# A two-layer block on one core: down products one chunk later, the second batch's norm ahead of the first mixer, attention's additions behind a gated value

## The chip, the cores and the metric

The kernel runs on one core of a Trainium2 chip. The metric is device time in microseconds (us) for one execution. The kernel before takes 360.51 us (median of three runs, 360.42 to 360.6). TensorE (PE in the profile) multiplies matrices, VectorE (DVE) and ScalarE (ACT) do elementwise work, GpSimd (POOL) does a few small powers, SyncE (SP) issues nearly all the DMAs.

## The reference

Four batches of 512 rows of 256 values pass through two layers. Each layer is a layer norm, a "mixer" `s` and a feed-forward `g` that start from the same normed value, and `x + s * silu(g)`.

```python
xn = _layernorm(x)
s = _L0_attn_ref(xn, ...)        # one step of a linear recurrence from zero state, RMS norm, + xn
g = _silu(_L0_ffn_ref(xn, W1, W2, W3))
x = x + s * g
xn = _layernorm(x)
s = _L1_attn_ref(xn, ...)        # layer norm, causal softmax attention, output projection, + xn
g = _silu(_L1_ffn_ref(xn, W1, W2, W3))
x = x + s * g

def _ffn_ref(x, W1, W2, W3):     # hidden size 1024, both layers
    hidden = silu(x @ W1.T) * (x @ W3.T)
    return fwht(hidden) @ W2.T   # Walsh-Hadamard transform of the hidden values
```

## The kernel before

**Precision.** Every matrix operand is kept as a high and a low part (`hi` cast by ACT at L61, `lo = src - hi` by DVE at L62, in `split`). A product is then three products, high by high, high by low and low by high; `mm3` (L80) issues them. So each value that goes into a product costs one ACT cast and one DVE subtraction, and the low part is always the last to come.

**Layer 0.** Batches are numbered 0 to 3 here, as in the code. For each batch `ffn` (L461) runs over eight chunks of 128 hidden values: two up products into PSUM (names `f_<b>gu`, a gate and a linear one, a pool of three banks), silu on ACT (L522), the product of the two on DVE (L523, name `f_<b>h`, called the gate of the chunk here; it frees the bank of the linear product), a split into `f_<b>hh` and `f_<b>hl`, and `down`, whose twelve products per chunk accumulate in `f_<b>dn`. `down` of a chunk is issued `defer` chunks after its up products; `defer` is 1 for batches 1 to 3 and 8 for batch 0, where the weights of the down product are still being prepared. In the program text the up and down products stand one after the other, and a `Beside` object puts steps of other work into 16 slots between them: the mixer of the same batch, the norm and transposes of the next batch, the gate of the batch before, the preparation of weights.

`mixer(b)` (L709) multiplies the transposed normed value with one 256 by 256 matrix (tiles `o`, four blocks, two to a bank), copies and squares on ACT (L719, L721), takes the power on POOL (L724), scales four tiles on DVE (L726, names `osb`) and adds them into `xn` (L729). The layer's output is made by `gate`: silu of the down products (L692, names `g_<b>g`), times `xn` (L698), added to `x` (L700). `norm(0, b + 1)` reads the next batch, makes `xn`, transposes it on PE (`xt_<b>tp`) and splits it into `xt`.

**Who decides the order.** In layer 0 the order of the instructions on each engine is chosen by the framework's scheduler from its own estimates, with the program order and the explicit `after(...)` links as inputs. Each engine then runs its list strictly in that order, and waits on semaphores for what the others deliver. From the end of layer 0's last up product the order of PE is fixed by hand (`line["fixed"]`).

**Layer 1.** `ffn_s` (L556) does the up products of two hidden chunks at a time, in four steps `q`, in a Strassen-like scheme of seven block products into banks `g`, `l` and `z` (names `f_<b>gu<q>g` and so on; the same pool of three banks). At the end of a step ACT takes silu of `g` into `h0`, and DVE multiplies it with `l` (L668, `first["gate"]`), which frees the bank that the next step's `z` needs. Attention's parts stand between the block products in a hand-written list of places. `pv` (L853) multiplies softmax weights with values; after every second tile it adds two tiles of the result into `xn` on DVE (L871). `prep_s` loads weights, makes sums of blocks, splits them (names `sraw`, `ssum`, `sp`) and stores them to DRAM, from where `load_s` reads them back (`sw`).

Of the kernel before, what the change touches and what calls it, by code (L numbers as in the profile page):

```python
# [35 lines left out]
def kernel(ctx: ExitStack, tc: tile.TileContext, a: dict, out: bass.AP):  # L36
    nc = tc.nc
# [39 lines left out]
    def transpose(*args):  # L77
        return in_line(nc.tensor.transpose, *args)

    def mm3(o, terms):  # L80

        seq = [(l[0], r[0]) for l, r in terms]
        for l, r in terms:
            seq += [(l[0], r[1]), (l[1], r[0])]
        for n, (l, r) in enumerate(seq):
            ins = matmul(o, l, r, start=n == 0, stop=n == len(seq) - 1)
        return ins
# [128 lines left out]
    def sl(i):  # L216
        return slice(i * P, (i + 1) * P)
# [72 lines left out]
    def k_pairs(lhs, lcols, rhs, rcols):  # L290
        return [
            ((lhs[0][:, k, lcols], lhs[1][:, k, lcols]), (rhs[0][:, k, rcols], rhs[1][:, k, rcols]))
            for k in range(2)
        ]
# [166 lines left out]
    def ffn(name, xT, w13, w2, slot, defer=1, spare=(), parts=1, behind=False, tail=()):  # L461

        w2h, w2l = w2
        dn, outs, firsts = [], [], {}

        def down(c, hh, hl, tiles=range(NT)):
            if not dn:  # L470
                dn.extend(psum(f"{name}dn{i}", [P, 2, D], tag="dn", bufs=2) for i in range(2))
                outs.extend(dn[t // 2][:, t % 2, :] for t in range(NT))
            for t in tiles:
                o = outs[t]
                for n, (l, r) in enumerate(((hh, w2h), (hh, w2l), (hl, w2h))):
                    first = c == 0 and n == 0
                    stop = c == NH - 1 and n == 2

                    def one(start):
                        return matmul(  # L480
                            o, l[:, sl(t)], r[:, c, :], start=start, stop=stop, skip_group_check=True
                        )

                    if first and t % 2 == 1:
                        with tc.issue_after(firsts[t // 2].ins):
                            ins = one(False)
                    elif first:
                        ins = firsts[t // 2] = one(True)  # L490
                    else:
                        ins = one(False)
            return ins

        queue, gates, late = [], [], []
        for c in range(NH):
            with after(gates[-2] if behind and c >= 2 else None):
                wh, wl = w13(c // 2)
            gu = []
            for j in range(2):  # L500

                o = psum(f"{name}gu{c}_{j}", [P, S], **(DN[0] if behind and c == 1 else GU))
                cols = slice((c % 2) * D + j * P, (c % 2) * D + (j + 1) * P)
                gu.append((o, cols))
            for half in range(parts if c == 0 else 1):
                n = S // (parts if c == 0 else 1)
                ts_ = slice(half * n, (half + 1) * n)
                if parts == 1 or c:
                    for o, cols in gu:
                        last_up = mm3(o[:, ts_], k_pairs((wh, wl), cols, xT, ts_))  # L510
                    continue

                for n, (w, x) in enumerate(((wh, xT[0]), (wl, xT[0]), (wh, xT[1]))):
                    for o, cols in gu:
                        for k in range(2):
                            last_up = matmul(
                                o[:, ts_], w[:, k, cols], x[:, k, ts_],
                                start=n + k == 0, stop=n + k == 3,
                            )
            gu = [o for o, _ in gu]  # L520
            h = hid(f"{name}h{c}")
            first["silu"] = nc.scalar.activation(h, gu[0], AF.Silu)  # L522
            gates.append(nc.vector.tensor_tensor(h, h, gu[1], ALU.mult))  # L523
            first["gate"] = gates[-1]
            if c < len(spare):
                hh, hl = spare[c]
            else:
                hh = hid(f"{name}hh{c}", F32R)
                hl = hid(f"{name}hl{c}", F32R)
            if c < len(spare):  # L530
                nc.scalar.copy(hh, h)
                late.append((hl, h, hh))
            else:
                split(h, hh, hl)
            for _ in range(2 if c >= NH - 2 else 0):
                if late:
                    lo_, h_, hi_ = late.pop(0)
                    with after(gates[-1]):
                        nc.vector.tensor_tensor(lo_, h_, hi_.bitcast(F32), ALU.subtract)
            queue.append((c, hh, hl))  # L540
            ups = last_up if behind else None
            with after(gates[-1] if behind else None), after(ups):
                slot(2 * c)
            if len(queue) > defer:
                down(*queue.pop(0))
            with after(gates[-1] if behind else None), after(ups):
                slot(2 * c + 1)
        line["fixed"] = bool(tail)
        line["last"] = last_up
        for what in tail:  # L550
            what()
        for q in queue:
            down(*q)
        return dn
# [154 lines left out]
    def mixer(b):  # L709

        xn, xT, m = xns[0, b], xTs[0, b], first["m"]
        osb = t4(f"osb{b}", [P, NT, D])
        r = small(f"ssr{b}")
        junk = t2(f"junk{b}", [P, D])
        for i in range(2):
            o = psum(f"o0_{b}_{i}", [P, 2, D])
            for j in range(2):
                mm3(o[:, j, :], k_pairs(xT, sl(2 * i + j), m, ALLD))
            nc.scalar.copy(osb[:, 2 * i : 2 * i + 2, :], o)  # L719
            for t in (2 * i, 2 * i + 1):  # L720
                nc.scalar.activation(junk, osb[:, t, :], AF.Square, accum_out=r[:, t : t + 1])  # L721
            yield
        nc.vector.tensor_scalar(r, r, 1.0 / D, RMS_EPS, ALU.mult, ALU.add)
        nc.gpsimd.tensor_tensor(r, r, mhalf, ALU.pow)  # L724
        for t in range(NT):
            nc.vector.scalar_tensor_tensor(  # L726
                osb[:, t, :], osb[:, t, :], r[:, t : t + 1], nwb, ALU.mult, ALU.mult
            )
        nc.vector.tensor_tensor(xn, xn, osb, ALU.add)  # L729
        yield  # L730

    class Attention:
# [45 lines left out]
        def tq(self, j):  # L778
            b = self.b
            if j == 0:  # L780
                self.tqs = t4(f"tqh{b}", [P, 2, S], F32R), t4(f"tql{b}", [P, 2, S], F32R)
            o = psum(f"tq{b}_{j}", [P, S])
            mm3(o, k_pairs(first["wqk"], sl(j), self.xg, ALLS))
            split(o, self.tqs[0][:, j, :], self.tqs[1][:, j, :])

        def v(self, i, j):
# [66 lines left out]
        def pv(self, i):  # L853
            b, xn, pr = self.b, self.xn, self.prs[i]
            if i == 0:
                self.rden = small(f"rden{b}")
                with after(first["h1"]):
                    nc.vector.reciprocal(self.rden, self.den)
            if i % 2 == 0:
                self.o = psum(f"pv{b}_{i}", [P, 2, D])  # L860
            o = self.o[:, i % 2, :]
            mm3(
                o,
                [
                    (tuple(z[:, sl(j)] for z in pr), tuple(z[:, j, :] for z in self.vs))
                    for j in range(i + 1)
                ],
            )
            if i % 2:
                for t in (i - 1, i):  # L870
                    nc.vector.scalar_tensor_tensor(  # L871
                        xn[:, t, :], self.o[:, t % 2, :], self.rden[:, t : t + 1], xn[:, t, :],
                        ALU.mult, ALU.add,
                    )

    class Beside:

# [119 lines left out]
    for b in range(B):  # L997
# [4 lines left out]
            tasks.append((prep, 12))  # L1002
        if b:
            tasks.append((call(gate_all, f"g0_{b - 1}", dn, xns[0, b - 1], xs[b - 1]), 1))
        tasks.append((mixer(b), MIXER))
        if b + 1 < B:
            if b:
                load_x(b + 1)
            if b == 2:
                tasks.append((prep_s(0), 4))  # L1010
            tasks.append((norm(0, b + 1), NORM))
        if b == 0:
            early = w2_tile("early0"), w2_tile("early1")
            spare = [
# [18 lines left out]
        if b == 0:  # L1033
            dn = ffn("f0_0", xTs[0, 0], w13, w2, bg.slot, NH, spare, parts=2, behind=True)
        else:
            tail = [run(atts[0].tq, j) for j in range(2)] if b + 1 == B else []
            dn = ffn(f"f0_{b}", xTs[0, b], w13, w2, bg.slot, tail=tail)
        bg.finish()


# [146 lines left out]
```

## Time and profile before

| | |
|---|---|
| median of three runs | 360.51 us (360.42 to 360.6) |
| the profiled execution | 360.78 us, its span 359.0 us |
| PE busy | 352.4 us (98%), 2477 instructions |
| DVE busy | 287.5 us (80%), 597 instructions |
| ACT busy | 197.8 us (55%), 373 instructions |
| POOL busy | 20.8 us (6%), 22 instructions |
| DMA | 52.25 MB, mean 146 GB/s |

The span is the time from the first to the last instruction that the profile shows; 1.78 us of the profiled execution lie around it. The profiled execution is 0.27 us above the median. Names in the profile have some of their numbers left out: `f_1gu` is batch 1 of layer 0, `f_1gu2z` is bank `z` of step 2 of batch 1 of layer 1. The busy time of consecutive instructions overlaps: two DVE instructions of 0.68 us each can start 0.60 us apart.

### The profile page before, as it was taken

The numbers are of one execution on the slowest core, as the hardware profiler recorded it, in microseconds if no ns is written. First come the engines' busy times: TensorE is split into PE (matmuls) and PEld (weight loads), VectorE is DVE, ScalarE is ACT, GpSimd is POOL, SyncE is SP. The second block draws the span as 40 slices with busy tenths as digits, with TensorE's granted clock in tenths as the row PEclk, the third lists the DMA queues.
The fourth block names the chain that finished last, engine by engine and source line by source line (L and its number), as shares of the span: only waits on it lengthen the run. The fifth ranks groups of instructions, "written<-read, shape, count | busy, mean of one in ns | idle before, by whom it ended". The sixth has DMA issues, their size and how long they took to land.

```text
span 359.0 us, 6278 instructions
## 1 busy us (share of the span) xinstructions
PE 352.4 (98%) x2477; PEld 328.1 (91%) x2477; DVE 287.5 (80%) x597; ACT 197.8 (55%) x373; POOL 20.8 (6%) x22
## 2 busy tenths in 40 slices
PE   8999999999999999999999999999999999999995
PEld 6878998888988898888999999999999999999995
DVE  6899648998579938998886957989669997567645
ACT  3766156266463425674467655576555676556443
POOL 2000110300020210100110001100011000000000
PEclk9999999999999999999999999999999999999999
DMA  7925000301044316656256045572554655445501
GB/s 235 341 91 206 2 1 2 99 18 60 0 157 165 150 39 233 248 180 195 105 207 263 16 190 206 203 224 103 204 179 165 207 186 204 136 151 192 197 2 58
DMA packets 16285, 52.25 MB, mean 146 GB/s; under 512 B 1633, under 2 KB 7937, under 8 KB 16257
## 3 DMA queue, kind: packets, MB, share of 16 engines
q1 hardware_dynamic: 15968, 51.60, 40.9%
q8 instruction: 19, 0.31, 0.4%
q10 hardware_dynamic: 288, 0.26, 0.2%
q14 instruction: 10, 0.07, 0.1%
HBM read 42.40 MB, written 9.45 MB: 144 GB/s over the span
## 4 chain that ended last, share of the span: by engine, by line
PE 96%; DVE 2%; ACT 1%; issue 0%; DVEq 0%
PE f_1dn L70 6%; PE f_2dn L70 6%; PE f_1gu L70 6%; PE f_0gu L70 6%; PE f_2gu L70 6%; PE f_3gu L70 6%; PE f_3dn L70 6%; PE f_0dn L70 6%; PE sc L70 4%; PE pv L70 4%; PE o L70 3%; PE v L70 3%; PE tq L70 3%; PE warm L70 2%; PE w2ps L70 1%; PE pt L70 1%
## 5 line engine op out<-in xcount | busy, mean ns | idle before, releaser
L70 PE MATMUL f_1gu<-xt,w 128*128 128x512 f32 x96 | 24.9, 397 | 0.3 <-ACT xt L61 0.3
L70 PE MATMUL f_3gu<-xt,w 128*128 128x512 f32 x96 | 25.0, 396 | 0.0
L70 PE MATMUL f_2gu<-xt,w 128*128 128x512 f32 x96 | 24.8, 395 | 0.0
L70 PE MATMUL f_0gu<-xt,w 128*128 128x512 f32 (+1 forms) x108 | 24.3, 378 | 0.0
L70 PEld LDWEIGHTS f_0gu<-xt,w 128*128 128x128 f32 x108 | 18.4, 188 | 4.4 <-issue 1.0
L70 PEld LDWEIGHTS f_1gu<-xt,w 128*128 128x128 f32 x96 | 17.0, 188 | 3.6 <-ACT xt L61 0.5
L70 PEld LDWEIGHTS f_2gu<-xt,w 128*128 128x128 f32 x96 | 17.0, 188 | 3.0
L70 PEld LDWEIGHTS f_3gu<-xt,w 128*128 128x128 f32 x96 | 17.0, 188 | 2.9
L61 ACT CAST f_2hh<-f_2h 128x512 fp32r<-128x512 f32 x16 | 9.9, 622 | 15.4 <-DVE f_2h L523 12.3
L70 PE MATMUL f_3dn<-w2l,f_3hh 128*128 128x256 f32 x64 | 17.7, 281 | 0.0
L70 PE MATMUL f_3dn<-w2h,f_3hh 128*128 128x256 f32 x64 | 17.7, 281 | 0.0
L70 PE MATMUL f_1dn<-w2l,f_1hh 128*128 128x256 f32 x64 | 17.7, 282 | 0.0
L70 PE MATMUL f_2dn<-w2h,f_2hh 128*128 128x256 f32 x64 | 17.7, 282 | 0.0
L70 PE MATMUL f_1dn<-w2h,f_1hh 128*128 128x256 f32 x64 | 17.7, 281 | 0.0
L70 PE MATMUL f_2dn<-w2l,f_2hh 128*128 128x256 f32 x64 | 17.6, 281 | 0.0
L70 PE MATMUL f_3dn<-w2h,f_3hl 128*128 128x256 f32 x64 | 17.0, 282 | 0.0
L70 PE MATMUL f_1dn<-w2h,f_1hl 128*128 128x256 f32 x64 | 17.0, 281 | 0.0
L70 PE MATMUL f_2dn<-w2h,f_2hl 128*128 128x256 f32 x64 | 16.7, 281 | 0.0
L61 ACT CAST f_3hh<-f_3h 128x512 fp32r<-128x512 f32 (+1 forms) x17 | 10.0, 594 | 10.2 <-DVE f_3h L523 6.1
L61 ACT CAST f_1hh<-f_1h 128x512 fp32r<-128x512 f32 x16 | 9.9, 622 | 9.7 <-DVE f_1h L523 6.6
L62 DVE TENSOR_TENSOR f_2hl<-f_2h,f_2hh 128x512 fp32r<-128x512 f32 x16 | 10.9, 682 | 3.9 <-ACT f_2hh L61 3.8
L70 PE MATMUL f_0dn<-w2l,f_0hh 128*128 128x256 f32 x48 | 13.7, 286 | 0.0
(487 smaller groups left out, 1147.6 us busy)
## 6 DMA issues: line engine op xcount, KB each, us to landing
sw<-s SPq DMA_DIRECT2D x32, 896.0 KB, 6.4
s<-sp SPq DMA_DIRECT2D x8, 512.0 KB, 3.8
s<-sp SPq DMA_DIRECT2D x8, 384.0 KB, 2.8
w2raw<-in_w SPq DMA_DIRECT2D x4, 512.0 KB, 5.6
sraw<-in_w SPq DMA_DIRECT2D x4, 512.0 KB, 4.3
mrb<-there SPq DMA_DIRECT2D x4, 512.0 KB, 3.7
w13raw<-in_w SPq DMA_DIRECT2D x3, 512.0 KB, 7.1
x<-in_x SPq DMA_DIRECT2D x3, 512.0 KB, 3.6
```

Of the source, the lines that this page charges most:

```text
L61: h = nc.scalar.copy(hi, src)
L62: return h, engine.tensor_tensor(lo, src, hi.bitcast(F32), ALU.subtract)
L70: ins = call(*args, **kwargs)
```

## The change

The change alters no amount of work; the same instructions are issued in another order.

1. `mm3` issued the two low products of each term side by side; now it issues all that use the low part of one operand and then all that use the low part of the other. `late` says which operand's low part comes last: 0 (the default) the left one, 1 the right one. `late=1` is set for the up products of batches 1 to 3 and `tq`, where the right operand is the activation, and for the mixer, where the right operand is the weight.
2. Batch 0's background list has `norm(0, 1)` ahead of `mixer(0)`, with weight 0, where it had the mixer first.
3. `ffn` of batches 1 to 3 gets `defer=2`.
4. In `Attention.pv` the two additions into `xn` are issued behind the last `first["gate"]`.

```diff
-    def mm3(o, terms):
+    def mm3(o, terms, late=0):
         seq = [(l[0], r[0]) for l, r in terms]
-        for l, r in terms:
-            seq += [(l[0], r[1]), (l[1], r[0])]
+        for side in (1 - late, late):
+            seq += [(l[1 - side], r[side]) for l, r in terms]
...
-                        last_up = mm3(o[:, ts_], k_pairs((wh, wl), cols, xT, ts_))
+                        last_up = mm3(o[:, ts_], k_pairs((wh, wl), cols, xT, ts_), late=int(not behind))
...
-                mm3(o[:, j, :], k_pairs(xT, sl(2 * i + j), m, ALLD))
+                mm3(o[:, j, :], k_pairs(xT, sl(2 * i + j), m, ALLD), late=1)
...
-            mm3(o, k_pairs(first["wqk"], sl(j), self.xg, ALLS))
+            mm3(o, k_pairs(first["wqk"], sl(j), self.xg, ALLS), late=1)
...
             if i % 2:
-                for t in (i - 1, i):
-                    nc.vector.scalar_tensor_tensor(
-                        xn[:, t, :], self.o[:, t % 2, :], self.rden[:, t : t + 1], xn[:, t, :],
-                        ALU.mult, ALU.add,
-                    )
+                with after(first["gate"]):
+                    for t in (i - 1, i):
+                        nc.vector.scalar_tensor_tensor(
+                            xn[:, t, :], self.o[:, t % 2, :], self.rden[:, t : t + 1], xn[:, t, :],
+                            ALU.mult, ALU.add,
+                        )
...
-        tasks.append((mixer(b), MIXER))
+        if b:
+            tasks.append((mixer(b), MIXER))
         if b + 1 < B:
             if b:
                 load_x(b + 1)
             if b == 2:
                 tasks.append((prep_s(0), 4))
-            tasks.append((norm(0, b + 1), NORM))
+            tasks.append((norm(0, b + 1), NORM if b else 0))
+        if b == 0:
+            tasks.append((mixer(b), MIXER))
...
-            dn = ffn(f"f0_{b}", xTs[0, b], w13, w2, bg.slot, tail=tail)
+            dn = ffn(f"f0_{b}", xTs[0, b], w13, w2, bg.slot, 2, tail=tail)
```

## The prediction

> **What bounds the kernel now.** I read the engines' busy time first, then the chain of waits, then PE's own waits, then DVE's timeline at the places that the change touches.
>
> ```profile
> PE 352.4 (98%) x2477; PEld 328.1 (91%) x2477; DVE 287.5 (80%) x597; ACT 197.8 (55%) x373; POOL 20.8 (6%) x22
> ...
> PE 96%; DVE 2%; ACT 1%; issue 0%; DVEq 0%
> ```
>
> PE carries 96% of the chain that ended last. The change leaves the number of instructions of every engine as it is, so time can come or go only where PE waits. These are all the waits of PE that the waits view lists:
>
> ```profile
> PE warm L70 <- DVE zr L924: 1.4, 1, 1.4
> PE f_0gu2z L70 <- DVE f_0h L668: 0.6, 1, 0.6
> PE f_1gu L70 <- ACT xt L61: 0.3, 1, 0.3
> ```
>
> The columns are total, times and longest, in us. The first is the start and untouched. So the most that the change can win is small, and the question is whether reordered work makes PE wait elsewhere. DVE in batch 1 of layer 0 decides that:
>
> ```profile
> 49.63 1.67 DVE L726 SCALAR_TENSOR_TENSOR osb<-osb,ssr,nwb 128x256 f32<-128x256 f32 x4 [1.12 <-POOL ssr L724]
> 51.34 1.23 DVE L729 TENSOR_TENSOR xn<-xn,osb 128x1024 f32<-128x1024 f32 x1
> ...
> 53.68 1.28 DVE L698 TENSOR_TENSOR g_0g<-g_0g,xn 128x512 f32<-128x512 f32 x2
> 54.88 1.28 DVE L700 TENSOR_TENSOR x<-x,g_0g 128x512 f32<-128x512 f32 x2
> 57.16 0.69 DVE L523 TENSOR_TENSOR f_1h<-f_1h,f_1gu 128x512 f32<-128x512 f32 x1 [0.99 <-ACT f_1h L522]
> 57.77 0.68 DVE L151 TENSOR_TENSOR w2b<-w2raw 128x512 f32<-128x512 f32 x1
> ...
> 64.11 0.66 DVE L62 TENSOR_TENSOR f_1hl<-f_1h,f_1hh 128x512 fp32r<-128x512 f32 x1
> ...
> 64.85 0.65 DVE L523 TENSOR_TENSOR f_1h<-f_1h,f_1gu 128x512 f32<-128x512 f32 x1
> ...
> 66.62 1.66 DVE L726 SCALAR_TENSOR_TENSOR osb<-osb,ssr,nwb 128x256 f32<-128x256 f32 x4
> 68.21 0.68 DVE L151 TENSOR_TENSOR w2b<-w2raw 128x512 f32<-128x512 f32 x1
> ...
> 69.41 0.68 DVE L62 TENSOR_TENSOR f_1hl<-f_1h,f_1hh 128x512 fp32r<-128x512 f32 x1
> ...
> 71.91 1.22 DVE L729 TENSOR_TENSOR xn<-xn,osb 128x1024 f32<-128x1024 f32 x1
> ```
>
> Columns: start, busy time, instruction, how many, and in brackets the idle time before it. From 57.16 on no bracket appears: DVE has no gap. The mixer of batch 0 and its gate (the first four lines) are done before that, in a stretch where DVE had idle time.
>
> **What goes: the boundary of batches 0 and 1.** The first up product of batch 1 starts at 51.79; the row before it started at 51.18 and holds the array for about 0.12, so PE stood for 0.49, and the next products came 0.1 late: 0.60 in all. It waited for the ACT cast of `xt` (51.15 + 1.08 for two), as the transposes stood at 49.82 to 51.0. In the compiled order of the kernel after, the norm's transposes stand at about 44.8 to 46.1, behind `xn`, which DVE had made by 43.2 before. The cast is done five us early. −0.60.
>
> **What goes: layer 1.** DVE here adds attention's two tiles before the gate of the chunk:
>
> ```profile
> 193.61 0.87 DVE L871 SCALAR_TENSOR_TENSOR xn<-pv,rden,xn 128x256 f32<-128x256 f32 x2
> 194.40 0.68 DVE L668 TENSOR_TENSOR f_0h<-f_0h,f_0gu1l 128x512 f32<-128x512 f32 x1
> ```
>
> Silu's output is there at 193.47 (ACT row, 192.88 + 0.59), so the gate can start at 193.60 and end at 194.28. PE's last transpose before `f_0gu2z` began its group of four at 194.03; four of 0.11 end at 194.47, and the product started at 195.22. The wait of 0.75 goes. In batches 1 and 2 `f_1gu2z` started at 241.75 and `f_2gu2z` at 288.32, both 0.14 after their gates ended (241.60, 288.18). There the low part of the other chunk (start 240.33) would go first, as soon as its cast is done (239.51 + 0.62 = 240.13), and the gate ends at 241.43 and 288.01: −0.17 each. In batch 3 the gate starts 0.03 earlier: −0.03. Sum −1.12. The additions themselves come 0.7 later on the same engine; behind them stand the low part of `pt` and the tile sums, where DVE was idle for 0.5 (at 197.35 and 242.13), and the bank that they free is next wanted at 243.24, a microsecond after they end. Cost nothing; without that idle time at most 0.1 each.
>
> **What comes: batch 1 on DVE.** In the compiled order the mixer of batch 0 now ends with `o` immediately ahead of batch 1's first up product (its second half at 49.75 to 51.16). So `osb` of batch 0, its addition into `xn`, the two products with `g` and the two additions into `x` all come behind the gate of chunk 0 on DVE. By the starts above that is 1.59 (taken from 66.62 to 68.21) + 1.14 (51.34 to 52.48) + 1.20 + 1.20 = 5.13. That gate itself comes earlier: twelve up products of 0.232 from 51.16 end at 53.95, so it starts at 54.07, not 57.16: 3.09. From there DVE has no gap, and runs 5.13 − 3.09 = 2.04 behind its old times. PE meanwhile is 0.60 early. Compare with the slack in the trace of before:
>
> - Low part of chunk 1: it ended at 64.77, PE used it at 67.81. In the new order `osb` of batch 1 (1.59) stands ahead of it and the additions into `x` (1.20) behind it: 64.77 + 2.04 + 0.39 = 67.2, wanted at 67.81 − 0.60 = 67.2. A stall of 0 to 0.2.
> - Gate of chunk 2, which frees the bank for `gu4`: 65.50 + 2.04 + 1.59 − 0.15 (two small aggregates go behind it) = 68.98; `gu4` started at 68.76, now 68.16 at best. Stall 0.8 to 1.0.
> - Low part of chunk 2: 70.09 + 2.04 + 1.14 (the addition of `osb` of batch 1 now goes ahead of it) = 73.27; wanted at 72.00 − 0.60 = 71.40. The total stall grows to 1.9, or 2.1 if I place the use by the new order's own count of PE work.
>
> After that the moved work is done: DVE is 2.0 behind its old times and PE 1.4, while the next pairs had 2.2 to 3.1 of slack, so nothing more follows here. I take +2.0. Bounds: 0.8 (only the bank of chunk 2 bites) to 2.5; not below nothing, as no wait is removed in this stretch.
>
> The Trainium skill, "VectorE: DVE Perf Modes", section "The DRAIN you can't avoid", says that the next op doesn't start until the pipeline is empty. The rows contradict it for these instructions: 57.16 and 57.77 are 0.61 apart with 0.69 busy. Summed with whole durations, the moved work would be 5.45 and the stall about 0.3 longer. The starts are what I sum.
>
> **What comes: batch 2.** `defer=2` hardly moves the down products: in the compiled order the scheduler puts `f_1dn` at the same places among the up products. What moves is small work beside them. In batch 2 two sums of `ssum` (113.09 to 113.43 and 113.52 to 113.83, 0.65) and the low part of `sp` (114.65 to 115.49, 0.84) go ahead of the low part of chunk 2, which ended at 113.17 and was used at 114.14: 1.49 − 0.97 = +0.5 if DVE and PE are shifted alike. On ACT a cast that waits for the load of `sraw` (110.98, `[1.14 <-DMA sraw<-in_w]`) goes ahead of the `hh` of that chunk. Bounds 0 (the load comes by its own time, and PE arrives 1.4 later) and 0.85 (PE reaches that place 0.3 sooner in the new order).
>
> **What costs nothing.** The order in `mm3` has the same products; it lets the low part of `xt` and `tq`'s input come two products later. In batch 3 the load of the last `sraw` is issued on SP behind a `sw` load that waits for PE until about 156; it would land near 162, and its first user on the way to PE has until about 168; if it landed 2 us later, it would cost as much as it is late. POOL's power for batch 0's mixer (1.0) is within the 54.07 above.
>
> **Sum.** −0.60 − 1.12 + 2.0 + 0.5 = +0.8. The profiled execution of 360.78 would become 361.6; on the median, 360.51, that is **361.3 us**. About 0.2% (0.7 us) is what a measurement of this kernel can tell from no change.
>
> **Clock.** PE waited 0.6 twice, and the row of granted clock stays at 9 in every slice. The Trainium skill, "TensorE: Matmul & The Clock Gate", section "HAM oscillation — how this bites in real kernels", says that idle gaps over about 3.4 us drop the clock to half, and the section "A second HAM failure mode: psum-queue depth-cycling" that frequent short idling can too. No run here shows such a gap; the three stalls are each under 1.1, so I add nothing. If the clock did drop for one such window, the kernel would lose some 1.7 more, by that page an estimate.
>
> **Rivals.**
> - *Batch 2 absorbs (0.25).* The batch 1 stall occurs, but it gives DVE, ACT and the load 1.4 more before batch 2, and nothing is late there: +0.3, 360.8. For it: DVE has idle time from 87 to 105. Against: the pile in batch 2 hangs on batch 2's own mixer, which PE's delay shifts too.
> - *No new stall (0.22, faster).* The pile on DVE never reaches PE, because its slack is larger than I count or because the down products really come a chunk later: −1.72, 358.8; with batch 2's 0.5, 359.3. It decides if DVE catches up by 2 us before 71.4. Against: the unbroken row of DVE starts, and the unmoved places of `f_1dn` (a chunk later would give about 4 us: twelve up products of 0.232 and twelve down products of 0.118).
> - *Everything at its upper bound (0.08).* A stall of 2.5 in batch 1 and 0.85 in batch 2: +1.6, 362.1; the mechanism is DVE's lag of 2.04 growing by 0.5 through ACT casts that themselves wait.
>
> **How the numbers follow.** My forecast has 0.45, with 360.7 to 362.0 as its own range; four fifths of it lie above the bound. Slower: 0.36 of the forecast, 0.05 of the first rival, 0.08 of the last: 0.49. Within 0.2%: 0.09, 0.20 and 0.02: 0.31. Faster: 0.20. The range 358.8 to 362.0 takes in the faster rival's value and leaves the ends.
>
> **What would show it.** Right: no wait of PE `f_1gu <- ACT xt`, none of `f_0gu2z <- DVE f_0h`, and new waits of PE in batch 1 for DVE `f_1h` or `f_1hl` near 68 to 74, about 2.0 in all, with a smaller one near 114 to 117. Wrong: PE without a gap in batch 1, or `f_1dn` standing elsewhere, or waits for a DMA.

## The result and the profile after

The changed kernel takes 362.97 us (median of six runs, 362.93 to 363.21) against 360.54 (six runs, 360.3 to 360.63) on the same chip: 2.43 us more, a ratio of 1.0069 with a 95% interval of 1.0056 to 1.0082. The forecast was 361.3 with 358.8 to 362.0 as range. The sign was right, the time lies outside the range, and the loss is three times the forecast of 0.8.

The chain of what ended last and PE's own waits, after (columns of the waits: total us, times, longest):

```profile
PE 77%; DVE 13%; ACT 3%; DMA 2%; issue 2%; SPq 1%; DVEq 0%
```

```profile
PE warm L70 <- DVE zr L926: 1.4, 1, 1.4
PE f_1dn L70 <- DVE f_1hl L62: 0.8, 1, 0.8
PE f_1gu L70 <- DVE f_1h L524: 0.7, 1, 0.7
PE f_2dn L70 <- DVE f_2hl L62: 0.5, 1, 0.5
PE f_0dn L70 <- DVE early L540: 0.3, 1, 0.3
PE f_0gu L70 <- ACT f_0h L523: 0.2, 1, 0.2
```

The two waits that the change was expected to remove are gone (`f_1gu` on ACT `xt`, `f_0gu2z` on DVE `f_0h`). Four of the new ones are on DVE, one on ACT. DVE's part in the chain went from 2% to 13%.

The waits view shows less than PE loses, because the end of a matmul is counted as busy while the next one is missing. So I counted, in both traces, how far the start of each PE instruction lies behind the one before it, beyond what that one streams (0.232 us for 512 columns, 0.118 for 256, 0.109 for a transpose), and left out what both traces have:

| place | forecast | measured in the trace |
|---|---|---|
| boundary of batches 0 and 1 | −0.60 | −0.59 |
| layer 1, the four gates | −1.12 | −1.05 |
| batch 1 | +2.0 | +2.26 |
| batch 2 | +0.5 | +0.74 |
| batch 0 | not in the sum | +1.26 |
| sum | +0.8 | +2.6 |

The spans differ by 2.2 (359.0 and 361.2); the first 14 us, which the change doesn't reach, were 0.2 shorter in the profiled execution after, and the remaining 0.2 is spread over small differences, most of them in layer 1.

DVE's timeline of batch 1 after, the same work as in the lines of before (start, busy, instruction):

```profile
55.35 0.69 DVE L524 TENSOR_TENSOR f_1h<-f_1h,f_1gu 128x512 f32<-128x512 f32 x1 [1.00 <-PE f_1gu L70]
55.95 1.67 DVE L727 SCALAR_TENSOR_TENSOR osb<-osb,ssr,nwb 128x256 f32<-128x256 f32 x4
...
59.34 1.22 DVE L730 TENSOR_TENSOR xn<-xn,osb 128x1024 f32<-128x1024 f32 x1
...
62.69 1.27 DVE L699 TENSOR_TENSOR g_0g<-g_0g,xn 128x512 f32<-128x512 f32 x2
...
66.15 1.64 DVE L727 SCALAR_TENSOR_TENSOR osb<-osb,ssr,nwb 128x256 f32<-128x256 f32 x4
67.72 0.68 DVE L62 TENSOR_TENSOR f_1hl<-f_1h,f_1hh 128x512 fp32r<-128x512 f32 x1
68.32 1.29 DVE L701 TENSOR_TENSOR x<-x,g_0g 128x512 f32<-128x512 f32 x2
...
69.61 0.65 DVE L524 TENSOR_TENSOR f_1h<-f_1h,f_1gu 128x512 f32<-128x512 f32 x1
...
72.66 1.22 DVE L730 TENSOR_TENSOR xn<-xn,osb 128x1024 f32<-128x1024 f32 x1
...
73.86 0.68 DVE L62 TENSOR_TENSOR f_1hl<-f_1h,f_1hh 128x512 fp32r<-128x512 f32 x1
```

and PE's timeline where it waits for it, with batch 0's two visible waits:

```profile
24.07 1.20 PE L70 MATMUL f_0gu<-xt,w 128*128 128x512 f32 x4 [0.22 <-ACT f_0h L523]
...
40.39 0.50 PE L70 MATMUL f_0dn<-w2h,early 128*128 128x256 f32 x2 [0.29 <-DVE early L540]
...
70.32 1.67 PE L70 MATMUL f_1gu<-xt,w 128*128 128x512 f32 x6 [0.66 <-DVE f_1h L524]
...
74.60 0.38 PE L70 MATMUL f_1dn<-w2h,f_1hl 128*128 128x256 f32 x1 [0.76 <-DVE f_1hl L62]
```

The table's batch 0 is the sum of three waits: 0.49 at 24.07, 0.22 at 31.76, where PE stands for the cast of `wih` on ACT and the view lists nothing, and 0.55 at 40.39. For the last one the rows show why. Before, DVE made the low parts that `down` needs (`early`) ahead of the low part of the mixer's matrix (`ml`):

```profile
37.84 1.27 DVE L539 TENSOR_TENSOR early<-f_0h,early 128x512 fp32r<-128x512 f32 x2
...
39.27 0.65 DVE L62 TENSOR_TENSOR ml<-mps,mh 128x512 fp32r<-128x512 f32 x1
```

After, `ml` goes first, 0.60 of work, and PE stands 0.55:

```profile
38.39 0.68 DVE L62 TENSOR_TENSOR ml<-mps,mh 128x512 fp32r<-128x512 f32 x1
...
39.65 1.28 DVE L540 TENSOR_TENSOR early<-f_0h,early 128x512 fp32r<-128x512 f32 x2
```

The first mixer's scalings, its addition, the gate's products and the additions into `x` now stand between the gates of batch 1, where before they lay ahead of the first. DVE runs from 55.35 to 74.5 without a bracket, and its numbers sit 1.2 to 1.3 behind those summed in the prediction, because batch 0 itself ended later: PE's first up product of batch 1 starts at 52.28, not 51.16, and the first gate at 55.35 against 54.07.

### The profile page after: what moved, and what is told of

It is laid out like the page before. It is cut to its first block, busy times and chain, and to the rows that moved or that the text cites. A ratio compares the mean times of both kernels' runs of the same rounds, so it can differ in the third digit from the quotient of the medians.

```text
span 361.2 us, 6272 instructions
## 1 busy us (share of the span) xinstructions
PE 353.0 (98%) x2477; PEld 327.3 (91%) x2477; DVE 286.8 (79%) x597; ACT 197.3 (55%) x373; POOL 18.1 (5%) x22
## 4 chain that ended last, share of the span: by engine, by line
PE 77%; DVE 13%; ACT 3%; DMA 2%; issue 2%; SPq 1%; DVEq 0%
PE f_3gu L70 6%; PE f_3dn L70 6%; PE f_0dn L70 5%; PE f_1dn L70 5%; PE f_2dn L70 5%; PE sc L70 4%; PE pv L70 4%; PE v L70 3%; PE f_1gu L70 3%; PE f_2gu L70 3%; PE tq L70 3%; DMA w13raw<-in_w 2%; PE o L70 2%; DVE osb L727 1%; DVE w2b L153 1%
## 5 line engine op out<-in xcount | busy, mean ns | idle before, releaser
L62 DVE TENSOR_TENSOR f_3hl<-f_3h,f_3hh 128x512 fp32r<-128x512 f32 (+1 forms) x17 | 11.0, 654 | 3.8 <-ACT f_3hh L61 3.6
```

Of the source, the lines that this page charges most:

```text
L62: return h, engine.tensor_tensor(lo, src, hi.bitcast(F32), ALU.subtract)
```

## The experiments

Theory A: the moved norm does the damage; it pushes the first mixer's work onto DVE in batch 1 and spoils batch 0. Theory B: the new order in `mm3` or the later `down` does it, through the order that the scheduler makes of them. The edits below are against the kernel before or after, as said. Ratios are to the kernel before on the same chip; three chips were used, on which the kernel before took 360.54 to 360.64. Waits of a batch that stand in no view are counted start to start, as in the table above.

**Attention's additions alone** (before, with only part 4):

```diff
+                with after(first["gate"]):
+                    for t in (i - 1, i):
...
```

> The kernel before with part 4 alone (attention's additions behind the gate). All theories: the four waits of PE for the gate in layer 1 go, and nothing else changes: 1.1 us less than before, 359.4. If the additions come too late for something behind them, less than that.

Measured: 359.36, ratio 0.9967 (0.9954 to 0.998). PE's waits:

```profile
PE warm L70 <- DVE zr L925: 1.5, 1, 1.5
PE f_1gu L70 <- ACT xt L61: 0.3, 1, 0.3
```

All four waits of layer 1 are gone and the boundary's is untouched. The term of −1.12 holds, and the additions cost nothing behind them.

**The norm not moved** (after, with the task list of before):

```diff
-        if b:
-            tasks.append((mixer(b), MIXER))
+        tasks.append((mixer(b), MIXER))
...
-            tasks.append((norm(0, b + 1), NORM if b else 0))
-        if b == 0:
-            tasks.append((mixer(b), MIXER))
+            tasks.append((norm(0, b + 1), NORM))
```

> The changed kernel with part 2 undone (first mixer ahead of the norm again), parts 1, 3 and 4 kept. Theory A (the moved norm pushes the first mixer's work onto DVE in batch 1 and spoils batch 0's order): the new waits of PE in batch 0 (1.1) and batch 1 (2.3) go, the wait at the boundary of 0.6 comes back, batch 2's 0.7 stays: 363.0 - 3.4 + 0.6 = 360.2. Theory B (the order in mm3 or the later down products make the waits, through the scheduler's new order): stays near 363, or at 363.6 with the boundary's wait.

Measured: 359.47, ratio 0.9969 (0.9957 to 0.9981), 0.7 less than theory A expected. With the norm in its old place, the order in `mm3` and `defer=2` together make no wait at all: batches 0 and 1 are clean, the boundary's wait is back (0.80 by start to start), and batch 2's is gone too. So batch 2's wait goes with the moved norm, too; theory B falls, as far as it says that parts 1 and 3 do it by themselves. In DVE's timeline of this run the low part of batch 2's chunk 2 is back in front of the sums:

```profile
112.60 0.66 DVE L62 TENSOR_TENSOR f_2hl<-f_2h,f_2hh 128x512 fp32r<-128x512 f32 x1
113.18 0.42 DVE L329 TENSOR_TENSOR ssum<-sraw 128x256 f32<-128x256 f32 x1
```

while after it stands behind them:

```profile
114.96 0.42 DVE L330 TENSOR_TENSOR ssum<-sraw 128x256 f32<-128x256 f32 x1
115.30 0.42 DVE L331 TENSOR_TENSOR ssum<-sraw 128x256 f32<-128x256 f32 x1
...
115.79 0.93 DVE L62 TENSOR_TENSOR sp<-sraw,sp 128x768 fp32r<-128x768 f32 x1
...
116.79 0.66 DVE L62 TENSOR_TENSOR f_2hl<-f_2h,f_2hh 128x512 fp32r<-128x512 f32 x1
```

**The moved norm with its weight of 3** (after, `NORM if b else 0` put back to `NORM`):

> The changed kernel with the moved norm's weight put back from 0 to 3, so that the background work of batch 0 is paced as before. Theory A1 (batch 0's new waits come from the pacing): 1.1 less than the changed kernel, 361.9, with batch 1's 2.3 unchanged. Theory A2 (they come from the norm standing ahead of the mixer, whatever its weight): 363.0.

Measured: 360.01, ratio 0.9983 (0.9974 to 0.9993): 2.96 less than the changed kernel, where 1.1 was expected if pacing mattered, with batch 1's 2.3 unchanged. Batch 0 loses 0.37, batch 1 0.32, batch 2 0.46. So the weight of 0 is the larger half of the damage, and not in batch 0 only. The code says how: a slot runs steps until `total * (k + 1) / slots` are done. With weight 0 the total is 15 for 18 real steps, so three steps, the mixer's, are left for the last slot, where `finish` runs whatever remains. With weight 3 `osb` starts at 52.30, ahead of batch 1's first gate; with weight 0 at 55.95, behind it:

```profile
52.30 1.67 DVE L726 SCALAR_TENSOR_TENSOR osb<-osb,ssr,nwb 128x256 f32<-128x256 f32 x4 [1.12 <-POOL ssr L724]
54.01 1.23 DVE L729 TENSOR_TENSOR xn<-xn,osb 128x1024 f32<-128x1024 f32 x1
55.15 0.68 DVE L523 TENSOR_TENSOR f_1h<-f_1h,f_1gu 128x512 f32<-128x512 f32 x1
```

**The moved norm alone** (before, with only part 2):

> The kernel before with part 2 alone (norm ahead of the first mixer, weight 0). Theory A: the boundary's 0.6 goes, batch 0's 1.1 and batch 1's 2.3 come, batch 2 and layer 1 are as before: 360.5 + 2.8 = 363.3. Theory B: 0.6 less than before, 359.9.

Measured: 365.38 (364.35 to 366.12), ratio 1.0131 (1.011 to 1.0152), 2 us worse than expected. Part of that is the clock: the two longer executions, 365.81 and 366.12, have a mean granted clock of 0.995 and 0.993, the two shorter, 364.35 and 364.94, have 1.0 and are 1.0 to 1.6 worse than expected. PE's waits in the execution of 364.94, beside the start's:

```profile
PE f_1dn L70 <- DVE f_1hl L62: 2.0, 1, 2.0
...
PE f_3dn L70 <- DVE f_3hl L62: 0.7, 1, 0.7
PE f_2dn L70 <- DVE f_2hl L62: 0.5, 1, 0.5
PE f_1gu L70 <- DVE f_1h L523: 0.3, 1, 0.3
PE f_0dn L70 <- DVE w2l L62: 0.2, 1, 0.2
PE f_0gu2z L70 <- DVE f_0h L668: 0.2, 1, 0.2
```

The loss is there without `mm3` and `defer`, and larger: 2.8 in batch 1, and 1.0 at the end of batch 3. So parts 1 and 3 shield PE from part of what part 2 does.

**Less for DVE to do** (after, without three of the four scalings of batch 0's `osb`; that part of the result is left unscaled):

```diff
-        for t in range(NT):
+        for t in range(NT if b else 1):
             nc.vector.scalar_tensor_tensor(
...
```

> The changed kernel without three of the four scalings of osb of the first mixer (part of the computation is left out: three quarters of batch 0's mixer are not scaled). DVE has 1.2 us less to do ahead of batch 1's products, PE has the same work. Theory A (DVE's pile of moved work makes PE wait): the waits of PE in batch 1 fall from 2.3 by about 1.2 and the kernel takes 361.8. Theory B (PE's new order or ACT makes them): 363.

Measured: 361.59, ratio 1.003 (1.0018 to 1.0041), 1.38 less than the changed kernel. In batch 1 PE stands 1.22 instead of 2.26, so 1.04 of the 1.2 us taken from DVE come back on PE; the rest of the gain is in batch 2 (0.45 instead of 0.74). DVE's pile is what PE waits for, nearly us for us.

**The weight of 0 in the old order** (before, norm still behind the mixer, its weight 0 in batch 0):

> The kernel before, mixer ahead of the norm as it was, with the norm's weight 0 in batch 0. Theory P (the weight slows the pace of the background list, so that its last steps fall behind the last chunk): new waits of PE in batch 0 of up to 0.5, a longer wait at the boundary (the transposes and the norm come last here), 361 to 362. Theory O (only the order matters): 360.5.

Measured: 360.99 (360.61 to 361.55), ratio 1.0014 (1.0005 to 1.0023). It costs 0.45, the lower end of the 361 to 362 expected. New waits stand in batch 0, 1.2 in the profiled execution, which is the longest of the ten (361.55); the boundary's wait did not grow (0.50). The weight does its large damage only together with the norm in front, because then the mixer is what is left over.

**Quicker pace in the old order** (before with part 4 and the norm's weight 6 in batch 0):

> A candidate for the best: the kernel before with attention's additions behind the gate, mixer still ahead of the norm, and the norm's weight 6 instead of 3 in batch 0, which quickens the pace: in the compiled order the mixer's products end 4 us and the norm's transposes 4 us sooner. Theory P: the boundary's 0.6 goes too, with no pile on DVE in batch 1: 359.4 - 0.6 = 358.8. Theory O: 359.4, or slower by new waits in batch 0.

Measured: 360.60, ratio 1.0002 (0.9993 to 1.0011). A miss: the boundary's wait went, but the scheduler's order of the later batches changed too.

```profile
PE f_3dn L70 <- DVE f_3hl L62: 0.6, 1, 0.6
PE f_1gu L70 <- DVE f_1h L523: 0.3, 1, 0.3
PE f_2dn L70 <- DVE f_2hl L62: 0.3, 1, 0.3
```

**The changed kernel with the old order in `mm3`**:

> The changed kernel with the old order of products in mm3. If the order of the low products and the new defer each shield PE from late low parts, this lies between the changed kernel (363.0) and the moved norm alone less the gain in layer 1 (365.4 - 1.2 = 364.2). At 363.0 the defer alone does it, at 364.2 the order in mm3 alone.

Measured: 362.62 (362.54 to 363.88), ratio 1.0066 (1.0052 to 1.008), below both expected ends. Batch 1 stands 2.83 instead of 2.26, so the order shields there by 0.6; but batch 0 stands 0.34 instead of 1.26. Batch 0's waits thus need the new order in `mm3` as well as the moved norm with weight 0: without any one of the three they are 0 to 0.6. The wait near 40 us goes with the place of `ml`: of the eight kernels with the norm in front, it stands in the four where DVE makes `ml` ahead of `early` (after, weight 3 with and without the order in `mm3`, and less scaling), and in none of the other four. No edit moved `ml` by itself, and whether `defer=2` has a part in batch 0's waits no run tells. Beside the moved norm alone, this kernel has no wait at the end of batch 3; that is what `defer=2` buys.

**Four candidates** that place the first mixer's work on DVE as early as before, or keep it so:

> The changed kernel, norm still ahead of the first mixer, with the norm's weight 5 in place of 0, which quickens batch 0's pace: in the compiled order the scalings of osb, the addition into xn and the gate's products of batch 0 stand ahead of the gate of batch 1's first chunk on DVE, as in the kernel before. Theory A (place of that work on DVE decides): no pile in batch 1, at most 0.3 of waits in batches 0 to 2, boundary and layer 1 gains kept: 358.8 to 359.2. Theory B (any norm ahead of the mixer costs): 360 as with weight 3, or more.

> The same without the new order in mm3. Theory A: 358.8 to 359.4; the low part of the activations is wanted earlier, which may cost a few tenths in batch 1. If mm3's order is what disturbs batch 0, this is the faster of the two.

> The kernel before, mixer ahead of the norm, with attention's additions behind the gate, defer 2 and the norm's weight 6. With defer 1 (the earlier run of weight 6) PE waited 0.85 in batch 3, 0.5 in batch 2 and 0.5 in batch 1. If the later down products give the low parts time, batch 3's wait goes and perhaps half of the others: 359.3. If defer does nothing for the order of PE, 360.6 as with defer 1.

> The changed kernel with the norm's weight 3 and the old order in mm3. With mm3's order this took 360.0, with 0.37 of waits in batch 0, 0.32 in batch 1 and 0.46 in batch 2. If mm3's order disturbs batch 0, batch 0's goes: 359.6. If it shields batch 1, batch 1's grows: 360.3.

Measured, in this order: 359.98 (ratio 0.9982, 0.9973 to 0.9992), 359.89 (0.9979, 0.9969 to 0.9988), 359.80 (0.9975, 0.9966 to 0.9985) and 360.11 (0.9986, 0.9976 to 0.9995). With weight 5, `osb` starts at 50.24 and the first gate of batch 1 at 55.09, behind most of the mixer's work, and PE has no wait in batch 1: there the place on DVE decides, as theory A says. But 0.58 came up in batch 0 and 0.46 in batch 2, so that the time, 359.98, is theory B's 360 and not theory A's 358.8 to 359.2:

```profile
PE f_0gu L70 <- DVE f_0h L523: 0.3, 1, 0.3
PE f_2dn L70 <- DVE f_2hl L62: 0.2, 1, 0.2
```

The third has `defer=2` where the run with weight 6 had 1, and its wait in batch 3 (0.86 by start to start) is gone, as expected; batch 1's (0.53) and batch 2's (0.52) stay, so it takes 359.80 and not 359.3. Without the order in `mm3`, weight 3 takes 360.11 against 360.01: no difference that the intervals show. None of the four reaches 359.36. Attention's additions alone (0.9967) and the changed kernel with the norm left where it was (0.9969) are the best versions found; their intervals don't tell them apart, nor the third candidate (0.9975) from either. Both lie 0.3% below the kernel before.

## Why the prediction was right or wrong

- *Boundary, −0.60.* Right: 0.59, and it stays away wherever the norm is moved or quickened.
- *Layer 1, −1.12.* Right: 1.05 in the trace, 1.2 by the median of the additions alone.
- *Batch 1, +2.0.* Right in mechanism and size: 2.26, and confirmed by taking work off DVE. The 0.26 is within the bounds given. The times that it starts from were wrong, as PE came to batch 1 0.49 late and not 0.60 early; but DVE and PE were late by nearly the same (1.3 and 1.1 against the sum), so the difference held. From the first gate to the end of the low part of chunk 2 the sum by starts has 19.20 (54.07 to 73.27), the trace 19.19 (55.35 to 74.54).
- *Batch 2, +0.5.* Right in the row and its pile, 0.74 within the bound of 0.85. Wrong in the heading under which it stood: I told it after `defer=2`, and the runs show that it comes with the norm's move or its quicker pace (0.52 with the mixer in front and weight 6, with `defer` 1 and 2 alike), and not with `defer` or `mm3`.
- *"What costs nothing."* This is the step that failed. It prices the order in `mm3`, the last load and POOL, and says nothing of batch 0 itself, where the moved norm acts first; the sum had no term and the range no bound for it. It was 1.26 in the trace, half of the measured loss of 2.43; without it the time would be about 361.7. The rest of the miss of 1.7 is the 0.26 and 0.24 of batches 1 and 2. Batch 0's order differs from its start, and could be read from the compiled order as batch 1's was: in the trace four `w2ps` products stand in a row from 17.79, where there were two at 18.05 and two at 20.32; a gate of a chunk stands at 23.15 on DVE, where it stood at 22.07; and `ml` stands ahead of `early`. I compared slack only from batch 1 on.
- *"`defer=2` hardly moves the down products."* Right for batches 1 and 2 (`f_1dn` stands at the same places among the up products in both traces). Wrong for batch 3: its first `down` product stands behind 36 up products, before behind 24, and with the moved norm of weight 0 or the quickened norm a wait of 0.9 to 1.0 comes at its end with `defer=1` and not with 2.
- *The rivals.* No stall on PE (0.22) and batch 2 absorbing (0.25) both fell. The last, with everything at its bound, came nearest at 362.1 and had 0.08; that is luck, as batches 1 and 2 stayed inside their bounds and the missing time lay in batch 0.
- *Spacing on DVE.* To sum by starts was right, but the rows don't contradict the Trainium skill: the section "The DRAIN you can't avoid" that the prediction cites also says "A next op that is not held starts earlier".
- *Clock.* Nothing to add was right for the changed kernel: its six executions have a mean granted clock of 0.999 to 1.0.

**Open.** Why the scheduler puts batch 2's sums ahead of the low part when the norm of batch 0 is moved or quickened (but not when it is slowed, with weight 0 in the old order) was not tried. Nor is it shown why the scheduler moves `ml`, or what delays the silu and the cast on ACT behind the other two waits of batch 0.

## What to carry to other kernels

When a step moves in a background list, price first the stage it moves within, and then every stage after it; a kernel that is 98% bound by one engine loses whatever the others are late, nearly us for us. Look at what a weight does to the pace of the rest: a weight below the real number of steps leaves the last steps for the last slot. Bundle less: the part that is worth something (attention's additions, −1.2 us) was buried under one that cost three times as much (the moved norm with weight 0, 3.5 us between 359.47 and 362.97).

## What the runs showed of the hardware

PE stood for 1.96 us at one place of the moved norm alone, and in the profiled execution the row of granted clock stayed at 9 in every slice. But not every execution of that kernel kept its clock. Two of its four have a mean granted clock of 0.995 and 0.993 and are 0.9 to 1.8 us longer than the two at 1.0; one of the four of the kernel with the old order in `mm3` has 0.995 and takes 363.88, where the others take 362.54 to 362.70 at 0.999 to 1.0. These are the two kernels in which PE stands about 2 us at one place; every other execution on record has 0.997 or more. By an estimate, a mean that is 0.5% lower over 363 us is 1.8 us lost on an engine that bounds the kernel, so the clock can account for the longer times. That the stall lowered it is not shown, as no profile of these three executions was kept. The Trainium skill, "TensorE: Matmul & The Clock Gate", section "HAM oscillation — how this bites in real kernels", has as its rule no idle gaps of PE over about 3.4 us; no run here has a gap that long.

DVE's starts stayed 0.60 apart at 0.68 busy through 19 us without a gap. With whole durations for the moved work in place of the spacing (5.45 for 5.13), the stretch of 19.19 above would have been put 0.3 too long.
